# Per-row weights of a gathered history: the SBUF tile of their sums replaced by 16 columns of a PSUM tile

## The chip, the cores and the metric

The kernel runs on one NeuronCore of a Trainium2 chip. The metric is the device time of one launch in microseconds, as the median of several runs. The time before the change is 36,713.39 us, the median of three runs that lie between 36,705.22 and 36,721.51 us.

## The reference

The kernel scores 16,384 users by an attention over their histories of 200 items each. Every history item is a row of 64 numbers in an embedding table of some 100,000 rows. Cut to what the change touches:

```python
it = i_emb[item]                       # (16384, 64)
h = i_emb[hist]                        # (200, 16384, 64), the gathered rows
feat = concatenate([h, it, h - it, h * it], axis=-1)
a = dice(feat @ au_W1 + au_b1, au_alpha, axis=1)
w = a @ au_W2 + au_b2                  # one weight per history row
cur = jnp.sum(w * h, axis=0)           # weighted sum over the 200 rows of a user
```

`dice(x)` is `x * (p + alpha * (1 - p))` with `p = sigmoid((x - mean) / sqrt(var))`; mean and variance are taken over the 16,384 users. Three small dense layers on `[u, it, c, cur]` follow, with dice over the users, and give two numbers per user. All is float32.

## The kernel before

**Tiling.** A step `k` handles 2,048 of the 16,384 users for one history position: 16 rows in each of the 128 partitions (`TD` = 16). Eight steps (`ND`) make one history position, and 200 positions make 1,600 steps. A loop of seven turns covers 24 positions each; the last 32 positions are written out behind it.

**A table made ahead.** The part of the first layer that depends on the history row alone is linear, so a prologue computes it once for every row of the item table and stores a table in HBM whose rows hold 128 numbers: the row itself (`D` = 64) and its product with the weights. The item's own part is kept in `xi`. Only the part for `h * it` is left for the main loop.

**The gather.** `fetch(k)` (L381) fills one of twelve buffers `land` by `gather` (L210), which issues 16 indirect DMAs on GpSimd (L213). Each of them takes its 128 row numbers from one column of an `idx` tile in SBUF, one number per partition, and brings one row of 512 bytes into each partition. 25,600 such instructions are issued in the main part, and 384 more in the prologue.

**A step.** `step(k)` (L462) is an order written out by hand and interleaves several steps:

- `turn(k-1)` (L386): VectorE transposes the gathered rows in blocks of 32 by 32 into the PSUM tile `ph` (L390), multiplies `ph` by the item rows into `hx` (L391), and transposes the second half of the rows (L392). `product` then runs 8 matmuls (L244) onto a PSUM tile `px`, which ScalarE has preloaded from `xi` (L476).
- `gates(k-10)` (L401): ScalarE computes the sigmoid and the dice factor into the PSUM tile `pg` (L405, L410). At every eighth step, `moments` computes mean and variance ahead of it.
- `weigh(k-10)` (L415): VectorE multiplies `pg` by the hidden values (L417) and transposes the product back (L418). It then sums each row's 64 values to one weight, 16 weights per partition (L420), computes (weight + bias) times the row (L425), and adds that to the sum `cur` (L429).
- `hidden(k-2)` (L394): VectorE adds `px` and the second half of the rows (L397), and takes their statistics (L399).

`pg` and `ph` are single PSUM tiles of 1,024 float32 per partition, used by every step; in the steps of the main part `ph` is written and read by VectorE alone. The line of the change is in `weigh`: the tile `r` of 16 weights comes from the SBUF pool `small` (two buffers); it is written at L420 and read at L425, where the rows (`land`) and the bias are read from SBUF too.

Of the kernel before, what the change touches and what calls it, by code (L numbers as in the profile page):

```python
# [8 lines left out]
F32 = mybir.dt.float32  # L9
# [5 lines left out]
P = 128  # L15
# [14 lines left out]
def din_kernel(  # L30
# [27 lines left out]
    TD = 2 * CD // P  # L58
# [6 lines left out]
    small = ctx.enter_context(tc.tile_pool(name="small", bufs=2))  # L65
# [40 lines left out]
    for a in range(P // S):  # L106
        r = ts(a, S)
# [9 lines left out]
    for a in range(P // S):  # L117
        for q, (a0, n) in enumerate(parts):
            r, u = slice(a * S, a * S + n), slice(a0, a0 + n)
# [21 lines left out]
    ph = psum.tile([P, CD], F32, name="ph")  # L141
# [81 lines left out]
    def halves(t, n=TD):  # L223

        return t.rearrange("p (e n t) -> p e n t", e=2, t=S)[:, :, :n]
# [123 lines left out]
    with ExitStack() as main:  # L349
# [25 lines left out]
        def by_row(t):  # L375
            return t.rearrange("p (n d) -> p n d", d=D)

        def x_of(k):
            return of_rows(land[k % LAND][:, :, D:])
# [35 lines left out]
        def weigh(k):  # L415

            nc.vector.tensor_mul(halves(pg), halves(pg), x_of(k))  # L417
            nc.vector.transpose(x_of(k), halves(pg))  # L418
            r = small.tile([P, TD], F32, tag="r", name="r")
            nc.vector.tensor_reduce(  # L420
                r, land[k % LAND][:, :, D:], mybir.AxisListType.X, ALU.add
            )
            c = k % ND
            rows = land[k % LAND][:, :, :D]
            nc.vector.scalar_tensor_tensor(  # L425
                by_row(pg), r.unsqueeze(2).to_broadcast([P, TD, D]), au_bias2, rows,
                ALU.add, ALU.mult,
            )
            nc.vector.tensor_add(cur[:, ts(c, TD)], by_row(pg), cur[:, ts(c, TD)])  # L429
# [32 lines left out]
        def step(k, last=None):  # L462
# [24 lines left out]
            if has(k - 10):  # L487
                if k % ND == 2:
                    moments((k - 10) // ND)
                gates(k - 10)  # L490
                weigh(k - 10)
# [208 lines left out]
```

## Time and profile before

| what | value |
|---|---|
| median of three runs | 36,713.39 us |
| profiled execution, its own time | 32,925.16 us |
| its span, first to last instruction | 32,922.9 us |
| GpSimd (POOL) busy | 24,717.0 us (75%) |
| VectorE (DVE) busy | 20,486.1 us (62%) |
| TensorE (PE) busy | 9,897.1 us (30%) |
| ScalarE (ACT) busy | 7,127.0 us (22%) |
| DMA traffic | 2,681.59 MB, mean 81 GB/s |
| granted TensorE clock, mean | 0.632 of full speed |

The busy time of an engine counts only while an instruction is recorded as executing; what lies between two records of the same engine is idle time, and the profile names what ended it. "issue" means that nothing visible was waited for. In the table of groups, a row gives source line, engine, operation, output and inputs, the number of instructions, their summed busy time in microseconds and the mean of one in nanoseconds. The profiled execution is a run of its own: its time is not one of the three that make the median.

### The profile page before, as it was taken

What the parts mean: (1) busy time and instruction counts of PE and PEld (TensorE: products, weight loads), DVE (VectorE), ACT (ScalarE), POOL (GpSimd) and SP (SyncE); (2) the same over time, 40 slices, a digit from 0 to 9 for tenths busy, and PEclk for the clock granted to TensorE, in tenths of its full rate; (3) what the DMA queues carried; (4) which work ended last, traced back from release to release, by engine and by line L of the source; (5) the groups of instructions that cost most, each with busy time, mean ns of one, the idle gap of its engine ahead of it and who ended that gap; (6) DMA issues with size and microseconds to landing.
All of it is one profiled execution on the core that took longest, in us unless ns stands there. A gap on an engine that the chain in (4) does not pass through costs nothing. (4 is left out here: it accounts for less than half of the span.)

```text
span 32922.9 us, 106947 instructions
## 1 busy us (share of the span) xinstructions
PE 9897.1 (30%) x13650; PEld 3847.8 (12%) x13650; DVE 20486.1 (62%) x21482; ACT 7127.0 (22%) x8732; POOL 24717.0 (75%) x25991
## 2 busy tenths in 40 slices
PE   4222222222222222222222222222222222223333
PEld 1111111111111111111111111111111111111111
DVE  5666666666666666666666666666666666666666
ACT  1222222222222222222222222222222222222222
POOL 7777777777777777777777777777777777777775
PEclk7666666666666666666666666666666666666666
DMA  5222222222222222222222222222222222223332
GB/s 161 80 79 78 79 78 79 79 78 78 79 79 79 79 78 79 79 78 78 79 79 79 79 79 78 79 79 78 78 80 79 78 80 78 79 79 88 92 92 66
DMA packets 1219178, 2681.59 MB, mean 81 GB/s; under 512 B 552540, under 2 KB 578684, under 8 KB 1212284
## 3 DMA queue, kind: packets, MB, share of 16 engines
q0 software_dynamic: 831488, 1691.97, 19.6%
q1 hardware_dynamic: 375228, 914.56, 9.0%
q10 hardware_dynamic: 11712, 67.98, 0.5%
q14 instruction: 635, 5.20, 0.1%
q8 instruction: 115, 1.88, 0.0%
HBM read 2599.36 MB, written 73.35 MB: 81 GB/s over the span
## 5 line engine op out<-in xcount | busy, mean ns | idle before, releaser
L213 POOL DMA_INDIRECT land<-table,idx x25600 | 24348.1, 951 | 7875.1 <-issue 7674.0
L244 PE MATMUL px<-hx,blk_m 128*128 128x512 f32 x12824 | 9453.7, 905 | 22727.6 <-DVE hx L391 20633.8
L390 DVE STREAM_TRANSPOSE ph<-land 128x1024 f32<-128x1024 f32 x1601 | 2016.5, 1259 | 10697.6 <-DMA land<-table,idx 10590.4
L244 PEld LDWEIGHTS px<-hx,blk_m 128*128 128x128 f32 x12824 | 3670.8, 301 | 28507.3 <-issue 23397.1
L476 ACT COPY px<-xit 128x1024 f32<-128x1024 f32 x1600 | 1626.6, 1017 | 22124.3 <-DVE land L397 22124.3
L405 ACT ACTIVATE pg<-land,fac 128x512 f32<-128x512 f32 x3220 | 2508.9, 779 | 85.8 <-DVE cur L429 25.0
L417 DVE TENSOR_TENSOR pg<-pg,land 128x1024 f32<-128x1024 f32 x1610 | 1939.0, 1204 | 925.2 <-ACT pg L410 925.0
L410 ACT ACTIVATE pg<-pg,au_al,au_1al 128x512 f32<-128x512 f32 x3220 | 2419.2, 751 | 106.6
L425 DVE SCALAR_TENSOR_TENSOR pg<-r,au_bias,land 128x1024 f32<-128x1024 f32 x1610 | 2085.1, 1295 | 56.7
L399 DVE BATCH_NORM_STATS2 st<-land 128x6 f32<-128x512 f32 x3204 | 2061.9, 685 | 54.3
L418 DVE STREAM_TRANSPOSE land<-pg 128x1024 f32<-128x1024 f32 x1610 | 2011.7, 1250 | 55.4
L429 DVE TENSOR_TENSOR cur<-pg,cur 128x1024 f32<-128x1024 f32 x1610 | 1970.7, 1224 | 55.0
L420 DVE TENSOR_REDUCE r<-land 128x16 f32<-128x1024 f32 x1610 | 1964.0, 1220 | 55.3
L391 DVE TENSOR_TENSOR hx<-ph,itT 128x1024 f32<-128x1024 f32 x1601 | 1960.3, 1224 | 56.2
L392 DVE STREAM_TRANSPOSE hx<-land 128x1024 f32<-128x1024 f32 x1601 | 1975.3, 1234 | 0.0
L397 DVE TENSOR_TENSOR land<-px,hx 128x1024 f32<-128x1024 f32 x1602 | 1945.1, 1214 | 0.0
L455 ACT ACTIVATE std<-var,eps 32x2 f32<-32x2 f32 x201 | 59.2, 295 | 2577.3 <-DVE var L451 2577.3
L405 ACT ACT_TABLE_LOAD x209 | 268.1, 1283 | 297.5 <-DVE fac L460 172.0
L244 PE MATMUL px<-rT,blk_h 128*128 128x512 f32 (+1 forms) x392 | 220.9, 726 | 168.2 <-DVE rT L295 168.2
L455 ACT ACT_TABLE_LOAD x201 | 257.9, 1283 | 3.5
L439 DVE COPY every<-mv 32x4 f32<-32x4 f32 x804 | 161.7, 201 | 15.2
L213 POOL DMA_INDIRECT land<-in_L_rec_i_emb,ids x128 | 126.4, 987 | 41.0 <-issue 38.6
(110 smaller groups left out, 1537.0 us busy)
## 6 DMA issues: line engine op xcount, KB each, us to landing
xit<-xi SPq DMA_DIRECT2D x1601, 512.0 KB
land<-table,idx POOLq DMA_INDIRECT x25600
table<-tab ACTq DMA_DIRECT2D x48, 1024.0 KB
tab<-in_L_rec_i_emb SPq DMA_DIRECT2D x48, 512.0 KB
zt<-uicT SPq DMA_DIRECT2D x48, 512.0 KB
idx<-in_r_hist SPq DMA_DIRECT2D x200, 64.0 KB
uicT<-t ACTq DMA_DIRECT2D x24, 512.0 KB
zbase<-zt SPq DMA_DIRECT2D x10, 512.0 KB
```

The source lines that it names most:

```text
L213: nc.gpsimd.indirect_dma_start(out=dst[:, n, :], out_offset=None, in_=rows, in_offset=bass.IndirectOffsetOnAxis(ap=ids[:, n : n + 1], axis=0),
L244: nc.tensor.matmul(dst[:, q * CH : q * CH + n], blk[:, e, q], rhs[:, e * CH : e * CH + n], start=(e == 0 and not onto), stop=(e == 1), ski ...
L390: nc.vector.transpose(halves(ph), of_rows(rows[:, :, :D]))
L391: nc.vector.tensor_mul(hm, ph, itT[:, k % ND])
L392: nc.vector.transpose(halves(hw), of_rows(rows[:, :, D:]))
L399: nc.vector.bn_stats(stats[l % 2][:, q, c, :], x_of(k)[:, q])
L405: nc.scalar.activation(halves(pg)[:, q], x_of(k)[:, q], AF.Sigmoid, bias=facs[i][:, 1, q : q + 1], scale=facs[i][:, 0, q : q + 1],)
L410: nc.scalar.activation(pg[:, ts(q, CH)], pg[:, ts(q, CH)], AF.Identity, bias=au_al[:, q : q + 1], scale=au_1al[:, q : q + 1],)
L418: nc.vector.transpose(x_of(k), halves(pg))
L420: nc.vector.tensor_reduce(r, land[k % LAND][:, :, D:], mybir.AxisListType.X, ALU.add)
L425: nc.vector.scalar_tensor_tensor(by_row(pg), r.unsqueeze(2).to_broadcast([P, TD, D]), au_bias2, rows, ALU.add, ALU.mult,)
L429: nc.vector.tensor_add(cur[:, ts(c, TD)], by_row(pg), cur[:, ts(c, TD)])
```

## The change

The 16 sums of a step are no longer written to a tile of their own in SBUF, but to the first 16 columns of the PSUM tile `ph`. The next instruction reads them from there. No instruction is added or removed, and the order on every engine is the same.

```diff
             nc.vector.tensor_mul(halves(pg), halves(pg), x_of(k))
             nc.vector.transpose(x_of(k), halves(pg))
-            r = small.tile([P, TD], F32, tag="r", name="r")
+            r = ph[:, :TD]
             nc.vector.tensor_reduce(
                 r, land[k % LAND][:, :, D:], mybir.AxisListType.X, ALU.add
             )
             c = k % ND
             rows = land[k % LAND][:, :, :D]
             nc.vector.scalar_tensor_tensor(
                 by_row(pg), r.unsqueeze(2).to_broadcast([P, TD, D]), au_bias2, rows,
                 ALU.add, ALU.mult,
             )
```

## The prediction

> **What bounds the kernel now.** I read the busy shares first, then the costliest groups, then the timeline of two steps. The page's first part gives busy microseconds, share of the span and count for each engine:
>
> ```profile
> PE 9897.1 (30%) x13650; PEld 3847.8 (12%) x13650; DVE 20486.1 (62%) x21482; ACT 7127.0 (22%) x8732; POOL 24717.0 (75%) x25991
> ```
>
> No engine looks full; GpSimd is nearest. The groups by line (busy us, mean ns of one, then idle time before them and what ended it) decide:
>
> ```profile
> L213 POOL DMA_INDIRECT land<-table,idx x25600 | 24348.1, 951 | 7875.1 <-issue 7674.0
> ...
> L390 DVE STREAM_TRANSPOSE ph<-land 128x1024 f32<-128x1024 f32 x1601 | 2016.5, 1259 | 10697.6 <-DMA land<-table,idx 10590.4
> ...
> L425 DVE SCALAR_TENSOR_TENSOR pg<-r,au_bias,land 128x1024 f32<-128x1024 f32 x1610 | 2085.1, 1295 | 56.7
> ```
>
> The gathers alone hold 24,348 us busy and 7,875 us between them, 32,223 of the 32,923 us span, and that time between them ends by "issue": GpSimd waited for nothing visible. VectorE idles 10,590 us for gathered rows. So GpSimd's rate of gathers sets the end, and VectorE follows. The timeline (start, duration in us, engine, what, idle before) shows how even that rate is, and where it is not:
>
> ```profile
> 16025.68 0.94 POOL L213 DMA_INDIRECT land<-table,idx  x1 [0.30 <-issue]
> 16026.59 1.25 DVE L418 STREAM_TRANSPOSE land<-pg 128x1024 f32<-128x1024 f32 x1
> 16026.93 0.94 POOL L213 DMA_INDIRECT land<-table,idx  x1 [0.30 <-issue]
> 16027.88 1.22 DVE L420 TENSOR_REDUCE r<-land 128x16 f32<-128x1024 f32 x1
> 16028.17 0.94 POOL L213 DMA_INDIRECT land<-table,idx  x1 [0.30 <-issue]
> 16029.13 1.29 DVE L425 SCALAR_TENSOR_TENSOR pg<-r,au_bias,land 128x1024 f32<-128x1024 f32 x1
> 16029.42 1.81 POOL L213 DMA_INDIRECT land<-table,idx  x1 [0.30 <-issue]
> 16030.46 1.22 DVE L429 TENSOR_TENSOR cur<-pg,cur 128x1024 f32<-128x1024 f32 x1
> 16031.53 0.94 POOL L213 DMA_INDIRECT land<-table,idx  x1 [0.30 <-issue]
> ...
> 16040.27 0.95 POOL L213 DMA_INDIRECT land<-table,idx  x1 [0.30 <-issue]
> 16041.49 1.29 DVE L425 SCALAR_TENSOR_TENSOR pg<-r,au_bias,land 128x1024 f32<-128x1024 f32 x1
> 16041.52 0.94 POOL L213 DMA_INDIRECT land<-table,idx  x1 [0.30 <-issue]
> 16042.77 0.95 POOL L213 DMA_INDIRECT land<-table,idx  x1 [0.30 <-issue]
> ```
>
> Gathers start every 1.25 us, whatever VectorE runs beside them, with one exception. The gather at 16029.42 starts 0.29 us after the product of L425 and takes 1.81 us in place of 0.94; it ends 0.81 us after that product. The product at 16041.49 started just ahead of a gather, and nothing was lengthened.
>
> I compared all starts of L425 with the gathers around them in the trace. A start 0.2 to 1.1 us after the start of a gather lengthens the next gather, by up to 1.0 us; one within 0.1 us on either side lengthens none. The cliff between the two is narrow: a start 1.05 us after a gather costs 1.00 us, one after 1.15 us costs nothing. In 253 of some 1,600 cases the next gather is longer by over 60 ns, 193 us in all. No other VectorE instruction of the step (L390, L391, L392, L397, L399, L417, L418, L420, L429) has a lengthened gather behind it in this way; L425 is the only long one with two inputs in SBUF besides the [128, 1] bias (`r` and `land`).
>
> **Profile against median.** The profiled execution took 32,925.16 us, 2.3 us more than its span. The median of the runs is 36,713.39 us, 3,788 us or 11.5% longer, while those three lie within 16 us of each other. Spread over 1,600 steps, that is 2.37 us a step. This is the open term of the sum. Something that costs nothing in the profiled execution costs 2.37 us a step in the others, and the only thing in the trace whose cost depends on the moment at which VectorE and GpSimd meet is L425[...].
>
> **The change, part by part.**
>
> *Against the profiled execution.* The lengthened gathers go: by the group's mean 25,600 x 0.951 less 25,600 x 0.944 (the median of one, and the 0.94 of the timeline) is 24,348.1 - 24,166.4 = 182 us; by the count above 193 us. Both lie on GpSimd's row, which sets the end, so 32,925 - 185 = 32,740 us. What is late next is the plain rate: 25,600 x 1.248 = 31,949 us, plus 489 us of prologue, 212 us behind the last gather, and about 75 us of pauses at the loop's turns, 32,725 us, which agrees.
>
> *L420 writes its 16 sums to PSUM, and L425 reads them there.* No such instruction is in the trace. Nearest rows: the transpose into PSUM (L390, 1,259 ns) against the same out of SBUF into SBUF (L392, 1,234) gives +25 ns for a write; for a read, L391 with one PSUM input takes 1,224 ns, as does L429, against 1,295 for L425 now. [...] I take the rows, -45 ns for the pair. By either, the sum is unchanged: VectorE idles 10,590 us / 1,600 = 6.6 us a step for rows, and this slack hides it[...].
>
> *`ph` gets a second use.* It is written and read by VectorE alone in these steps, and VectorE works in order: L391 has read `ph` before L420 writes it, L425 has read it before the next L390. No wait on another engine is added, no instruction and no DMA moves on any queue, and SyncE's and GpSimd's streams are untouched: nothing.
>
> [...] The row first: the lengthened gathers under L425, by at most some 1.0 us. [...]
>
> *Against the median.* The gain lies between 0 and 3,788 + 185 = 3,973 us. The lower part, 1,600 x 1.00 = 1,600 us, needs only that L425 falls on the wrong side of the cliff in every step. That is near: L425 follows the landing of a gather by a fixed chain (rows land, then L390, L391, L392, L417, L418, L420), and its starts heap up 0.1 us from the cliff. An execution in which that chain is 0.1 to 0.2 us shorter loses 1 us in every step. For the rest, the gather would have to be held about twice as long as the trace shows. I take the upper end as likeliest, since one cause that depends on timing explains a gap that exists only between differently timed executions, and I see no second one: the runs then fall to the profile's plain rate, **32,740 us**, -10.8%.
>
> **The rivals.**
>
> - *Lock only, no more than the trace shows.* The runs lie on the wrong side of the cliff: 0.2 to 1.3 us a step, 320 to 2,085 us off, centre 1.0 us, 35,100 us; the remaining 2,000 us have another cause that stays. For it: no block much over 1.0 us is in the trace. Against: it needs two causes.
> - *Small gain.* The gap belongs to the gather's rate in unprofiled runs (3,788 / 25,600 = 0.148 us each), and L425 costs what it costs in the profile: 36,713 - 190 = 36,520 us. For it: the evenness of the rate. Against: nothing in the trace says why profiling should quicken gathers.
> - *No change.* L425 never meets a gather in the runs[...]: 36,713 us.
> - *Slower.* In the unprofiled runs VectorE, not GpSimd, is the bound (place: L390 would no longer idle for rows). [...] It decides only from where 6.6 us of slack a step are gone; the profile shows them in every step, so this is unlikely.
>
> **How the numbers follow.** Chances: full recovery 0.45 (32,500 to 33,400 us); lock only 0.25; small gain 0.16; no change 0.09; slower 0.05. A change of 0.2% (73 us) is about what a measurement can tell. Small gain is nearly all beyond that; so faster 0.85, same 0.10, slower 0.05. The range reaches from 32,450 us (plain rate 1.237 us a gather, 0.9% quicker than in the profile) to 36,600 us, which takes in the lock cases and most of the small gains and leaves out no change and slower.
>
> **What would show it.** In the profile after: the group of L213 at a mean of 944 ns or little more, no gather over 1.1 us beside L425[...], L390 still idle for rows, a span near 32,735 us. The deciding number is not in the profile: the median must fall to within 1% of the profiled execution. If the gap stays near 3,788 us, the step that failed is the attribution of the gap to L425. [...]

## The result: no change, and a profile that differs from the one before

The changed kernel takes 36,714.58 us (median of 12 runs, 36,705.29 to 36,725.39), the kernel before 36,717.45 us in the 12 runs beside it. The ratio is 0.9999, with a 95% interval of 0.9991 to 1.0007. The forecast of 32,740 us and its range, which ended at 36,600 us, were wrong.

The profiled execution of the changed kernel took 36,716.59 us: it is one of the runs it stands for, which the profiled execution of the kernel before, with 32,925 us, was not. Its page has these rows (busy us, mean ns of one, then idle time before them and what ended it):

```profile
PE 9935.6 (27%) x13650; PEld 3862.9 (11%) x13650; DVE 20561.5 (56%) x21482; ACT 7130.4 (19%) x8732; POOL 27176.7 (74%) x25991
...
L213 POOL DMA_INDIRECT land<-table,idx x25600 | 26806.9, 1047 | 9101.4 <-issue 8715.3
...
L390 DVE STREAM_TRANSPOSE ph<-land 128x1024 f32<-128x1024 f32 x1601 | 2013.4, 1258 | 12102.5 <-DMA land<-table,idx 10814.2
...
L425 DVE SCALAR_TENSOR_TENSOR pg<-ph,au_bias,land 128x1024 f32<-128x1024 f32 x1610 | 2081.7, 1293 | 57.2
...
L420 DVE TENSOR_REDUCE ph<-land 128x16 f32<-128x1024 f32 x1610 | 1976.9, 1228 | 55.6
```

L425 now reads `ph`, as meant. But the gathers, expected at a mean of 944 ns, take 1,047 ns, and the time between them has grown as well. GpSimd's gathers still fill the span (26,807 + 9,101 us of 36,714), so the place of the bound is right and its rate is not. A stretch of 10,000 us in the middle shows the rate: the stretch, its length, the gathers' busy us and their number, granted clock, DMA share and GB/s. First the profiled execution of before, then the changed kernel.

```profile
5000.00:15000.00 10000.00, 7557.19 (x7948) 0.63 0.28 79
```

```profile
5000.00:15000.00 10000.00, 7538.48 (x7148) 0.61 0.26 71
```

That is a gather every 1.258 us in the one and every 1.399 us in the other. Over 25,600 gathers the difference of 0.141 us makes 3,600 us, which is nearly all of the gap of 3,788 us that the prediction set out to explain.

### The profile page after: what moved, and what is told of

Read it like the earlier page. It is cut to its first block, busy times and chain, and to the rows that moved or that the text cites. A ratio compares the mean times of both kernels' runs of the same rounds, so it can differ in the third digit from the quotient of the medians.

```text
span 36714.4 us, 106947 instructions
## 1 busy us (share of the span) xinstructions
PE 9935.6 (27%) x13650; PEld 3862.9 (11%) x13650; DVE 20561.5 (56%) x21482; ACT 7130.4 (19%) x8732; POOL 27176.7 (74%) x25991
## 3 DMA queue, kind: packets, MB, share of 16 engines
q0 software_dynamic: 831488, 1691.97, 17.7%
## 5 line engine op out<-in xcount | busy, mean ns | idle before, releaser
L213 POOL DMA_INDIRECT land<-table,idx x25600 | 26806.9, 1047 | 9101.4 <-issue 8715.3
L390 DVE STREAM_TRANSPOSE ph<-land 128x1024 f32<-128x1024 f32 x1601 | 2013.4, 1258 | 12102.5 <-DMA land<-table,idx 10814.2
L425 DVE SCALAR_TENSOR_TENSOR pg<-ph,au_bias,land 128x1024 f32<-128x1024 f32 x1610 | 2081.7, 1293 | 57.2
L420 DVE TENSOR_REDUCE ph<-land 128x16 f32<-128x1024 f32 x1610 | 1976.9, 1228 | 55.6
L460 DVE COPY fac<-fac 32x4 f32<-32x4 f32 x603 | 134.8, 223 | 304.6 <-issue 295.9
```

Source lines behind the costliest of these rows:

```text
L213: nc.gpsimd.indirect_dma_start(out=dst[:, n, :], out_offset=None, in_=rows, in_offset=bass.IndirectOffsetOnAxis(ap=ids[:, n : n + 1], axis=0),
L390: nc.vector.transpose(halves(ph), of_rows(rows[:, :, :D]))
L420: nc.vector.tensor_reduce(r, land[k % LAND][:, :, D:], mybir.AxisListType.X, ALU.add)
L425: nc.vector.scalar_tensor_tensor(by_row(pg), r.unsqueeze(2).to_broadcast([P, TD, D]), au_bias2, rows, ALU.add, ALU.mult,)
```

## The experiments

Two theories stood at the start. Theory A is the prediction's: in the runs, the two SBUF inputs of L425 hold the gathers for up to 2.4 us a step. Theory B: the gathers are slower in the runs for another reason, and L425 matters little. Each time below is one run; the kernel before, run beside each group, took 36,676 to 36,708 us, so differences of some 30 us mean nothing.

### The kernel before, profiled again

The kernel is unchanged.

> The kernel before, unchanged, profiled a second time. Theory A (in the runs, L425 with two inputs in SBUF holds the gathers): about 36,715 us, and the gathers that are longer than 944 ns stand behind starts of L425, some 2.4 us a step in all. Theory B (L425 has little to do with it; in the runs the gathers are slower for another reason that the first profiled execution did not have): about 36,715 us, with gathers of 1.09 us and more at other places of the step, as in the profile of the changed kernel, and 1.0 us or less a step behind L425. If 32,925 us comes back, the two times are two conditions of one kernel, drawn anew for each execution.

It took 36,683.31 us. Its gathers, from the page:

```profile
L213 POOL DMA_INDIRECT land<-table,idx x25600 | 27056.4, 1057 | 8838.3 <-issue 8605.8
```

and in the timeline of one step (start, duration in us; lines of other work left out):

```profile
16023.98 1.29 DVE L425 SCALAR_TENSOR_TENSOR pg<-r,au_bias,land 128x1024 f32<-128x1024 f32 x1
16024.08 2.00 POOL L213 DMA_INDIRECT land<-table,idx  x1 [0.30 <-issue]
...
16026.39 0.94 POOL L213 DMA_INDIRECT land<-table,idx  x1 [0.30 <-issue]
...
16030.13 1.34 POOL L213 DMA_INDIRECT land<-table,idx  x1 [0.30 <-issue]
16031.78 1.10 POOL L213 DMA_INDIRECT land<-table,idx  x1 [0.30 <-issue]
16033.18 1.09 POOL L213 DMA_INDIRECT land<-table,idx  x1 [0.30 <-issue]
```

Two kinds of long gathers stand here. The one of 2.00 us is held by L425. The gathers of 1.09 to 1.34 us further on have no L425 near them; they are the other reason.

The two kinds can be told apart. From 1.6 to 29.9 ms of the first profile, every gather behind a start of L425 that was longer by over 300 ns ended 0.80 to 0.82 us after L425 did. I call a gather held if it ends there and is longer than 944 ns by over 60 ns. In that stretch 219 of 1,405 starts of L425 hold the next gather in the first profile. Here 916 of 1,263 do, for 737 ns on average. Over the whole run that is 830 us, or 0.52 us a step. So the runs do lie on the costly side of the cliff, as the prediction suspected.

In the changed kernel no gather behind a start of L425 is over 1.2 us, and by that measure one of 1,263 is held, by 151 ns. The hold is gone. Yet the time is the same. From the profile taken again to that of the changed kernel, the gathers' busy time falls by only 250 us (27,056 to 26,807), and the idle time between them grows by 263 us (8,838 to 9,101). The gain was made and given back: 2,058 gathers of the changed kernel take over 1.2 us, none of them under L425, and 1,677 with VectorE idle for more than half of their time.

### More of the suspect, and none of it

```diff
-            nc.vector.scalar_tensor_tensor(
-                by_row(pg), r.unsqueeze(2).to_broadcast([P, TD, D]), au_bias2, rows,
-                ALU.add, ALU.mult,
-            )
+            for _ in range(3):
+                nc.vector.scalar_tensor_tensor(
+                    by_row(pg), r.unsqueeze(2).to_broadcast([P, TD, D]), au_bias2, rows,
+                    ALU.add, ALU.mult,
+                )
```

This edit was made on the kernel before and on the changed one; a third kernel is the one before without these lines.

> The kernel before with the product of L425 done three times in a row (the same result written three times, weights in SBUF). Theory A: each copy holds the gathers for up to 1.29 us, so two more copies add up to 2 x 1.29 x 1,610 = 4,150 us: 38,000 to 40,900 us. Theory B with a small lock: 36,715 to 37,300 us. VectorE has 6.6 us of slack a step, so its own 2.6 us more should add nothing.

> The changed kernel with the product of L425 done three times in a row (weights in PSUM). Theories A and B alike: no lock, 36,700 to 36,800 us; the difference to the same with weights in SBUF is the price of two SBUF inputs for three products a step. If both are equal, two SBUF inputs cost nothing in the runs.

> The kernel before without the product of L425 (the unweighted pg is added to cur instead). Theory A: the hold goes with it, about 32,900 us. Theory B: 36,600 to 36,720 us, since the gathers are slow for another reason.

They took 36,704.29, 36,713.54 and 36,678.05 us. Three products with weights in SBUF, three with weights in PSUM, and none at all: 35 us apart, about as much as runs of one kernel differ, where theory A asked for thousands. Theory A is refuted. The starts of the gathers show what is constant instead. I averaged them over the 128 gathers of each history position, for 16 positions of the first part of the loop: 1,400.0 ns in the kernel before profiled again (standard deviation 0.05 ns), 1,400.0 with three products from SBUF and also with none, 1,400.1 with three products from PSUM, 1,401.3 in the changed kernel. What is lost on one gather is made good soon after: behind the gather of 2.00 us above, the next ones start at 16026.39, 27.64, 28.89 and 30.13, 1.25 us apart, and behind held gathers this lasts until the average is 1.400 us again.

### What the pace belongs to

Four kernels leave work out of the changed kernel's main part. Their edits, one line or block each (where gathers are cut short or left out, twelve buffers in place of ten are also zeroed at the start):

```diff
 # e2_no_xit
-            nc.sync.dma_start(xit[k % XI], xi[c])
+            if k < XI:
+                nc.sync.dma_start(xit[k % XI], xi[c])
 # e2_half_rows
-            gather(land[k % LAND], idx[l % IDX][:, ts(c, TD)], table)
+            gather(land[k % LAND][:, :, :D], idx[l % IDX][:, ts(c, TD)], i_emb)
 # e2_no_gather: the gather's line is left out
 # e2_gathers_only: the gather's line stays, all else of step(k) is left out
```

> The changed kernel without the transfers of xi in the steps (512 KB each; only the first two of each turn of the loop are left, and the preload takes what lies in the buffer). The runs so far average 1.400 us a gather, whatever VectorE does. Theory P (each gather of 128 rows is paced at 1.40 us by itself): 36,700 us. Theory S (the pace is that of a path shared with the other transfers or with SyncE): faster, toward 25,600 x 1.248 us, 32,000 to 34,000 us.

> The changed kernel with gathers of half the bytes (rows of 256 bytes out of the item table, in place of 512 out of the made table; the same number of rows and instructions). Theory D (the pace of 1.40 us is that of the bytes moved): the gathers fall to their own 1.25 us, 32,500 to 33,500 us. Theory P or S (per instruction or per row): 36,700 us.

> The changed kernel without the gathers of the main part (all else runs on what lies in the buffers). Gives the bound of everything else: by the rows of the profile, VectorE has 12.9 us a step plus short waits, so 13.5 to 16 us a step, 22,000 to 26,000 us. If it stays above 32,900 us, GpSimd is not what sets the end in the runs.

> The changed kernel whose main part only gathers (no transfers of xi, no work of VectorE, ScalarE or TensorE in the steps). Theory P: 1.40 us a gather even alone, 36,000 to 36,700 us. Theory S or theory E (other engines' work slows the gathers): 1.25 us a gather, 32,400 to 32,900 us.

Without the transfers of `xi` it took 36,691.69 us, with rows of half the bytes 36,683.80, without gathers 22,155.68, with gathers only 36,506.60 us. So everything but the gathers needs 22,156 us. The gathers alone need nearly the whole time. The same stretch of 10,000 us in the last kernel (busy us and number of PE, PEld, DVE, ACT and POOL, then clock, DMA share and GB/s) has no other compute engine at work:

```profile
5000.00:15000.00 10000.00, 0.00 (x0) 0.00 (x0) 0.00 (x0) 0.00 (x0) 7737.25 (x7153) 0.50 0.17 47
```

Its timeline shows the pace setting in:

```profile
16005.85 0.94 POOL L213 DMA_INDIRECT land<-table,idx  x1 [0.30 <-issue]
16007.10 0.94 POOL L213 DMA_INDIRECT land<-table,idx  x1 [0.30 <-issue]
16008.35 1.06 POOL L213 DMA_INDIRECT land<-table,idx  x1 [0.30 <-issue]
16009.71 1.09 POOL L213 DMA_INDIRECT land<-table,idx  x1 [0.30 <-issue]
16011.11 1.09 POOL L213 DMA_INDIRECT land<-table,idx  x1 [0.30 <-issue]
16012.51 1.10 POOL L213 DMA_INDIRECT land<-table,idx  x1 [0.30 <-issue]
```

Behind a short delay a few gathers start every 1.25 us, with 0.94 us each, as in the first profile. Then each takes 1.09 us and they start every 1.40 us. The time before each stays at 0.30 us, ended by "issue", so nothing visible is waited for: the 0.15 us more lie within the gather. No backlog of transfers shows: by the DMA records, the first packet of a gather starts 0.71 us after the gather's end in this kernel (median) and 0.70 us in the first profile.

Two more kernels ask what the 1.400 us depend on: gathers into 64 partitions, and plain transfers of the same size in place of gathers.

```diff
 # e3_half_partitions
-            gather(land[k % LAND], idx[l % IDX][:, ts(c, TD)], table)
+            gather(land[k % LAND][:P // 2], idx[l % IDX][: P // 2, ts(c, TD)], table)
 # e4_plain_dma
-            gather(land[k % LAND], idx[l % IDX][:, ts(c, TD)], table)
+            for n in range(TD):
+                nc.gpsimd.dma_start(land[k % LAND][:, n, :], table[ts(n, P)])
```

> The changed kernel with gathers into 64 partitions in place of 128 (half the rows and bytes, as many instructions). Theory I (the pace of 1.400 us belongs to the instruction): 36,700 us. Theory R (it belongs to the rows or their descriptors, 128 x 10.9 ns): the pace falls to 0.7 us and the kernel to GpSimd's own time for half a gather, or to VectorE's 22,150 us at the least.

> The changed kernel whose 16 gathers a step are 16 plain transfers from GpSimd's queue (the same 128 rows of 512 bytes each, consecutive rows of the table instead of rows by number). Theory X (the pace of 1.400 us belongs to every transfer that GpSimd issues): again 1.40 us an instruction, 36,500 to 36,800 us. Theory Y (it belongs to the indirect form): GpSimd's own time for a plain transfer, or VectorE's 22,150 us at the least.

Half the rows took 36,704.10 us, and a gather of 64 rows still takes 1.402 us with the time before it ((26,691.2 + 9,212.0) us over 25,600). With half the bytes it was 36,683.80 us. So in these kernels the pace goes by the instruction, not by its rows or bytes. The plain transfers took 22,184.06 us. Their page:

```profile
PE 9919.9 (45%) x13650; PEld 3853.5 (17%) x13650; DVE 20317.1 (92%) x21482; ACT 7127.3 (32%) x8732; POOL 13905.4 (63%) x25991
...
L384 POOL DMA_DIRECT2D land<-table x25600 | 13535.7, 537 | 7857.8 <-issue 6898.1
```

25,600 transfers of 537 ns, and VectorE, at 92%, is the bound: the time is within 28 us of that without gathers. The number of DMA packets is no reason either: the page counts 831,488 on GpSimd's queue here, as with the gathers. So the pace showed with the indirect transfers (1.400 us) and not with the plain ones (0.84 us, (13,535.7 + 7,857.8) us over 25,600).

### The slack, and the change where there is none

If the pace holds, GpSimd has 16 x (1.400 - 1.249) = 2.4 us a step to spare, and only work beyond that costs time. So I gave it idle work behind the gathers of each of the 1,344 steps of the loop: one or four memsets on the changed kernel, and four on the kernel before.

```diff
             if has(k):
                 fetch(k)
+            if last is None:
+                for _ in range(4):
+                    nc.gpsimd.memset(zt[:, 0], 0.0)
```

> The changed kernel with one idle piece of work for GpSimd in each of the 1,344 steps of the loop (a memset of 1,024 numbers per partition, about 1 us, behind the 16 gathers). Theory P (in the runs the gathers are paced at 1.400 us each on average, and GpSimd, which needs 1.25 us, has 16 x 0.15 = 2.4 us a step to spare): nothing, 36,650 to 36,750 us. Theory G (GpSimd's own time sets the end): 1 x 1,344 = 1,300 us more, 38,000 us.

> The same with four such memsets, about 4 us a step. Theory P: the 2.4 us of slack are used up, (4 - 2.4) x 1,344 = 2,150 us more, about 38,900 us. Theory G: 5,400 us more, about 42,000 us.

> The kernel before (weights in SBUF) with the same four memsets. Once GpSimd has no slack left, the hold of the gathers by L425 must show: by the profile taken again it is about 0.6 us a step, so 0.4 to 1.0 us x 1,344 = 500 to 1,350 us more than the changed kernel with four memsets. If both are equal, the hold was not a cost even then. The memsets move the meeting points of gathers and L425, so the size is uncertain; the sign is not.

One memset (968 ns) took 36,786.00 us, 71 us above the changed kernel, where 1,300 us of GpSimd's time were added: nearly all of it hidden. Four took 38,675.84 us, 1,961 us above it or 1.46 us a step. Their own time is 5,138 us, 3.8 us a step:

```profile
L485 POOL MEMSET zt<- 128x1024 f32 x5376 | 5137.6, 956 | 231.7
```

So some 2.4 us a step were hidden, the slack worked out above.

The kernel before with four memsets took 39,673.77 us, 998 us or 2.6% more than the changed one with four. The pages of the two, changed kernel first:

```profile
L213 POOL DMA_INDIRECT land<-table,idx x25600 | 24417.7, 954 | 8092.1 <-issue 8004.9
```

```profile
L213 POOL DMA_INDIRECT land<-table,idx x25600 | 25455.5, 994 | 8062.4 <-issue 7967.1
```

The idle time is the same to 30 us, and the busy time of the gathers differs by 1,038 us, nearly the 998 us between the two times. The timeline of the second shows where (lines left out):

```profile
16013.01 1.29 DVE L425 SCALAR_TENSOR_TENSOR pg<-r,au_bias,land 128x1024 f32<-128x1024 f32 x1
16013.15 1.97 POOL L213 DMA_INDIRECT land<-table,idx  x1 [0.30 <-issue]
...
16015.42 0.94 POOL L213 DMA_INDIRECT land<-table,idx  x1 [0.30 <-issue]
...
16016.67 0.94 POOL L213 DMA_INDIRECT land<-table,idx  x1 [0.30 <-issue]
```

With GpSimd's own time as the bound, the other gathers shown take 0.94 us and only the one under L425 takes 1.97. From 1.6 to 29.9 ms, 977 of 1,149 starts of L425 hold the next gather by the measure above; in the changed kernel with four memsets none of 1,184 does. The hold costs 998 / 1,344 = 0.74 us a step, and the change removes it. The change does what it says; in the kernel as it stands the hold is paid out of slack.

## Why the prediction was wrong, step by step

- **The bound** (GpSimd's gathers) was right. Without them the changed kernel took 22,156 us.
- **The hold of a gather by L425**, its size of up to 1 us and its end by the weights in PSUM were right. With the weights in SBUF, in the kernel before profiled again, 916 of 1,263 starts of L425 held a gather, by 737 ns on average; with the weights in PSUM it was one of 1,263, by 151 ns. The pair with four memsets shows the same, 977 of 1,149 against none of 1,184. A held gather ends 0.81 us behind L425, as the prediction's own rows show. By what means L425 holds it was not shown.
- **The instructions' own cost** was close: L420 went from 1,220 to 1,228 ns (+25 by the prediction's row for a write), L425 from 1,299 in the profile taken again (1,295 in the first) to 1,293 (-71 by its row for a read). The pair cost +2 ns, not -45. VectorE's slack hides it, as forecast: L390 still idles 10,814 us for rows. The second use of `ph` added no wait: the idle time before L420 and L425 is 55.6 and 57.2 us in all, 55.3 and 56.7 in the first profile.
- **"Against the median"** is the step that failed. It put the 3,788 us between profile and runs down to L425, "since one cause that depends on timing explains a gap". The runs show a pace of 1.400 us for each gather, with no VectorE at work, in place of 1.249 us. The prediction's own count spoke against its choice: no gather in its trace was lengthened by much over 1.0 us, which makes 1,600 us in 1,600 steps, so a second cause of some 2,200 us was needed. (The 1.3 us at the top of its range for "lock only", and the 1.29 us expected of a copy of L425, are L425's own duration taken as the author's estimate.) The rival "small gain" had the right place and nearly the size, 0.148 us for each gather against 0.141 measured; its time of 36,520 us was still wrong, by the next point.
- **What lies on the path.** Even with the gap understood, subtracting 185 us from the median would have been wrong. The sum took every us of GpSimd's row as one of the end. Under the pace it is not: 0.52 us of holds a step went, other gathers became longer in their place, and nothing left the end. 2.4 us a step of that row are slack.
- **The rival "no change"** came true for another reason than it gave: in the kernel before profiled again L425 does meet gathers (916 of 1,263 starts), and still the time stayed when the changed kernel freed them.

What stays open: what sets 1.400 us, and why one profiled execution ran without it. It did not come back in any run here, so whether the change gains its 185 us in that condition was not seen. Nor is it shown what keeps the count; the traces show only that delays are made up at 1.25 us until the average is 1.400, and that the first packets start no later meanwhile (0.71 us against 0.70).

## What to carry to other kernels

If the profiled execution's own time is far off the median, as here by over 10%, its rows describe another condition. Take a profile whose time is that of the runs before weighing any row, and divide the gap by the counts of the bounding engine's instructions first. An engine whose instructions follow each other without a visible wait can still have slack: here 2.4 us a step were hidden in the gathers' own durations and gaps. Adding idle work to it measures the slack, and a gain smaller than that slack does not reach the end. A hidden gain can be made visible by using up the slack in both kernels and comparing those.

## What the runs showed of the hardware that was not expected

- Indirect gathers from GpSimd averaged 1.400 to 1.401 us an instruction in the six traces whose starts were averaged (the kernel before profiled again, those with three products or none, gathers only, the changed kernel), but 1.258 us in the first profiled execution. Over 128 gathers the average kept to 1,400.0 ns with a standard deviation of 0.05 ns in the kernel before profiled again. With rows of 256 bytes in place of 512 the time was 36,683.80 us, with 64 rows in place of 128 it was 36,704.10 us, against 36,714.58 us. Behind a delay, and in the first profiled execution, GpSimd started one every 1.25 us.
- The pace held as an average over thousands of gathers. At the loop's turn GpSimd pauses for some 26 us (24.9 to 27.2 in the changed kernel, 26.7 in the one with gathers only); behind one in the kernel before profiled again, the gathers ran ahead of 1.400 us by 25.3 us, that is about 170 gathers at 1.25 us, before the pace set in. In the kernel with gathers only, a whole turn of 3,072 gathers averages 1,400.0 ns with its pause included, so the pause cost nothing.
- Plain transfers of the same size from the same queue took 537 ns each and showed no such pace: from one to the next it was 0.84 us on average, with VectorE as the bound.
- The hold of a gather by L425 ended at the same distance each time: in the first profile and with four memsets, all gathers longer by over 300 ns behind a start of L425 (195 and 849, from 1.6 to 29.9 ms) ended 0.80 to 0.82 us after L425.
